# Latent attention in one program: when the stacked query copies are issued, and in which order Pool works

## The chip, the cores and the metric

The kernel runs on one core of a Trainium2 chip. The metric is the device time of one execution in microseconds (us). Engines are named as the profile names them: PE is TensorE's matmul and PEld its weight load, DVE is VectorE, ACT is ScalarE, POOL is GpSimd and SP is SyncE, which here issues DMAs only.

## The reference

One post-norm transformer layer on a sequence of S = 2048 rows of 512 features: multi-head latent attention with 16 heads, a residual and a layer norm, then one linear layer with scale and bias, a residual and a layer norm. Cut to what matters:

```
cq   = rms_norm(x @ w_qa.T)                      # 384 wide
q    = (cq @ w_qb.T)  -> 16 heads x (128 + 64)    # nope part, pe part
q_pe = rope(q_pe)                                 # 64 wide, per head
ckv  = x @ w_kva.T    -> latent 128 (rms_norm), k_pe 64 (rope, shared by all heads)
kv   = latent @ w_kvb.T -> k_nope, v per head
scores = (q_nope @ k_nope.T + q_pe @ k_pe.T) * 192 ** -0.5, causal
out  = softmax(scores) @ v ; x = layernorm(x + out @ w_o.T)
x    = layernorm(x + (x @ (weight * scale[:, None]).T + bias))
```

## The kernel before, in words

**Numbers.** fp32 values go through PE as a high and a low part in a rounded fp32 format, so that each product takes three matmuls. The probabilities are split into two f16 parts (high and low) in the same way. k_nope and v are absorbed: the scores are taken against the shared latent (Kn) and the shared rotary key (Kp), and the values are the latent (V); the heads' value matrices are multiplied into w_o at the end.

**Tiling.** The 16 heads are 8 pairs p. The queries are 4 blocks b of 512 rows, and each block has 4 query tiles qt of 128. In the profiled execution block 0 runs from 0 to about 260 us (with the projections of x and of the weights beside it), block 1 to about 480, block 2 to about 880, block 3 to about 1370; then come the output projection, the norms and the linear layer. The loop in `units` goes over p, qt and (from block 1 on) the two heads j of the pair. Names like (3,6,2) are block, pair, query tile; (0,1,1) beside ring copies is pair, query tile, head in block 1.

**One head (blocks 1 to 3).** `head_scores`: PE computes scores s (L438: three matmuls with Kn, two with Kp, and a mask matmul, L441), DVE takes maxima (L510) and the bias (L517/L518/L520), ACT takes exponentials into a buffer pr (L532) and sums them. `head_probs`: ACT casts pr to f16 (L563), Pool subtracts to get the low part (L564), and `turn` transposes both on DVE back into pr (L546) and issues four SP DMAs (L553) that place them in a ring, `ring<-pr`. `values`, some heads later and in two halves, multiplies the ring's tile with V (L619). In blocks 2 and 3 the result is multiplied by the inverse sums iv (DVE, L628) and stored (ot_d). The inverse comes by a detour through memory: `settle` sums, inverts and turns (DVE, L468, L469, L473), Pool stores it (`rows`, L476), and `values` has Pool load it spread over the partitions (`iv`, L612; the pool of iv has two buffers). In block 0 a pair is processed at once: L598 and L599 are its cast and subtraction.

**The stack.** `project_pe(b, g)` makes the rotary query parts of a group g of four heads. DVE leaves a high part in ph and a low part in prod, both with the heads along the partitions. Eight DMAs of 128 KB each, for head j = 0..3 and part i = high, low, copy 32 partitions at a time into the tile pe, where a head's high part and low part lie one above the other (L393 and L395). `score` reads pe in the matmuls with Kp. A group serves two pairs.

**Putting off.** In block 0 the loads and stores go to Pool's queue (`state["queue"]` is nc.gpsimd). From block 1 on it is nc.sync, and stores and stack copies wait in a list. The list is visited at the end of each `head_probs`, and emptied at the start of each pair:

```python
later.append([n, dst, src])         # put_off(dst, src, n), from block 1 on

def put_in(all=False):
    kept = []
    for n, dst, src in later:
        if n == 0 or all:
            nc.sync.dma_start(dst, src)          # L330
        else:
            kept.append([n - 1, dst, src])
    later[:] = kept
```

**Who sets the order.** In block 0 a scheduler with a planned timeline orders all engines. Engines named in `tc.manual_schedule(engines=...)` keep the program's order instead: PE and SP from block 1 on, DVE and ACT too from (3,0,1) to the end of block 3's hand-over (L729). Pool's order is the planner's throughout. Block 3 also fetches what the output stage needs: `prepare_output` in pairs 6 and 7 loads wv (L871), wo (L862), and two pairs' results with their inverse sums (`latent_load` L823, `latent_rows` L839), and splits them (`latent_split`, L849 on DVE, L64 on ACT, L65 on DVE); `accumulate` (L888) multiplies them.

Of the kernel before, what the change touches and what calls it, by code (L numbers as in the profile page):

```python
# [49 lines left out]
def mla_block(ctx: ExitStack, tc: tile.TileContext, a, out):  # L50
    nc = tc.nc
    ET = mybir.EngineType
# [8 lines left out]
    def split(ps, h, l, scale=None):  # L61

        if scale is None:
            nc.scalar.activation(h, ps, AF.Copy)  # L64
            nc.vector.tensor_tensor(l, ps, h.bitcast(F32), ALU.subtract)  # L65
        else:
            nc.scalar.activation(h, ps, AF.Copy, scale=scale)  # L67
            nc.vector.scalar_tensor_tensor(l, ps, scale, h.bitcast(F32), ALU.mult, ALU.subtract)  # L68
# [124 lines left out]
    def value_output(p, pool, tag):  # L193

        wvo = state["wvo"][p]
        for j in range(2):
            ps = pool.tile([P, HID], F32, tag=tag, name=f"ps_wo{2 * p + j}")
            nc.tensor.matmul(ps, state["wv"][:, 2 * p + j], state["wo"][2 * p + j], start=True, stop=True)  # L198
            split(ps, wvo[:, 0, j, :], wvo[:, 1, j, :], kvln_o)
            yield  # L200
# [118 lines left out]
    def put_off(dst, src, n=0):  # L319

        if state["queue"] is nc.gpsimd:
            nc.gpsimd.dma_start(dst, src)
        else:
            later.append([n, dst, src])
# [9 lines that stand above are left out]
# [20 lines left out]
    def load_wpe(b, g):  # L354
        if b == NB:
            return
        w = state["wpe", b, g] = prj.tile([P, 2, LT, 256], F32R, tag="wpe", name=f"wpe{b}_{g}")
        move(state["queue"], w, wpe_d[g])

    def project_pe(b, g, direct=None):  # L360

        if direct is None and ("wpe", b, g) not in state:
            load_wpe(b, g)
        w = state.pop(("wpe", b, g)) if direct is None else direct
        cq, cs = state["cq"], state["cs"]
        prod = prj.tile([P, 2, 2, QB], F32, tag="prod", name=f"prod{b}_{g}")
        for x in range(2):
            ps = psum["m"].tile([P, QB], F32, tag="m", name=f"ps_pe{b}_{g}_{x}")
            n = 0
            for lt in range(LT):  # L370
                for i, k in ((0, 0), (0, 1), (1, 0)):
                    nc.tensor.matmul(  # L372
                        ps, w[:, i, lt, x * P : (x + 1) * P], cq[:, k, lt, :], start=n == 0, stop=n == 8
                    )
                    n += 1
            for k in range(2):
                nc.vector.tensor_tensor(prod[:, k, x, :], ps, cs[:, k ^ x, :], ALU.mult)
            if x == 0:
                yield
            elif b or g == 3:  # L380
                load_wpe(*((b, g + 1) if g < 3 else (b + 1, 0)))
        rp, tp = prod[:, 0], prod[:, 1]
        nc.vector.tensor_tensor(rp[:, 0, :], rp[:, 0, :], rp[:, 1, :], ALU.subtract)
        nc.vector.tensor_tensor(rp[:, 1, :], tp[:, 0, :], tp[:, 1, :], ALU.add)
        ph, pl = prj.tile([P, 2, QB], F32R, tag="ph", name=f"ph{b}_{g}"), tp.bitcast(F32R)
        split(rp, ph, pl)
        pe = blk.tile([P, 4, QB], F32R, tag="pe", name=f"pe{b}_{g}")

        for j in range(4):
            for i, part in enumerate((ph, pl)):  # L390
                to, src = pe[64 * i : 64 * i + 64, j, :].bitcast(F32), part[32 * j : 32 * j + 32].bitcast(F32)
                if state["queue"] is nc.gpsimd:
                    nc.sync.dma_start(to, src)  # L393
                else:
                    put_off(to, src, 1)  # L395
        state["pe", b, g] = pe
        yield

# [24 lines left out]
    def project(b, p):  # L423
        if p % 2 == 0:
            yield from project_pe(b, p // 2)
        yield from project_nope(b, p)
# [215 lines left out]
    def drain():  # L642
        while fillers:
            fill()
# [48 lines left out]
    def flush():  # L693
        while probs:
            for _ in probs.pop():
                pass

    def units(pool, ring, b):
        lag = min(ring.shape[1] // (2048 * (b + 1)) - 1, 3) if b else 2

        for p in range(NPAIR):
            put_in(True)


            if p + 1 == NPAIR:
                at = (1, 2, 4, 5) if b < NB - 1 else (1, 3, 5, 7)
            elif p % 2 == 0 and p + 2 < NPAIR:
                at = (0, 1, 2, 3) if (b, p) == (1, 0) else (0, 1, 3, 4)
            else:
                at = (3, 4)  # L710
            if b and p % 2 == 0 and p + 2 < NPAIR:
                fillers.append(project_pe(b, p // 2 + 1))
            if p + 1 < NPAIR:
                fillers.append(project(b, p + 1) if b == 0 else project_nope(b, p + 1))
            elif b + 1 < NB:
                fillers.append(project(b + 1, 0))
            if b == NB - 1 and p == NPAIR - 1:
                ctx_p.close()
                pcr = state["pcr"] = ctx.enter_context(
                    tc.tile_pool(name="pcr", bufs=2, side="right", reuse_waits="tile")  # L720
                )
                state["wvo"] = [pcr.tile([P, 2, 2, HID], F32R, name=f"wvo{p}", bufs=1) for p in range(EARLY)]
                for i in range(EARLY):
                    fillers.append(value_output(i, psum["m"], "m"))
                at = (3, 4, 5, 6)
            for qt in range(4):
                nk = (4 * b + qt + 1) * P
                if (b, p, qt) == (NB - 1, 0, 1):
                    ctx_f.enter_context(tc.manual_schedule(engines={ET.PE, ET.SP, ET.DVE, ET.Activation}))  # L729
                if (b, p, qt) == (0, NPAIR - 1, 3):  # L730
                    s0, PT = -4 * nk, prj.tile([P, 4 * nk], F16, tag="ph", name="carry")
                elif b == 0:
                    s0, PT = -4 * nk, pool.tile([P, 4 * nk], F16, tag=f"PT{qt}", name=f"PT{p}_{qt}")
                else:
                    s0, PT = None, place(ring, 2048 * (b + 1), 4 * nk, (b, p) == (2, NPAIR - 1) and qt > 0)
                if nk <= 512:
                    pi = pair_scores(pool, b, p, qt, nk)
                    flush()
                    probs.append(pair_probs(pool, b, p, qt, nk, PT, pi))
                    if qt == 1:  # L740
                        settle((b, p))
                    fill()
                    next(side[0], None)
                    if p and qt % 2:
                        next(side[1], None)
                    if qt % 2:
                        next(side[0], None)
                    run_values(lag)
                    run_values(lag)
                else:  # L750
                    for j in range(2):
                        if 2 * qt + j == 1 if b < 2 else j == 0:
                            settle((b, p))
                        prepare_output(b, p, 2 * qt + j)
                        prev = probs.pop() if probs else iter(())
                        pi = head_scores(pool, b, p, j, qt, nk, prev)
                        probs.append(head_probs(pool, b, j, nk, PT, pi))
                        if (b, p, qt, j) == (1, 0, 1, 0):
                            half_values()
                            half_values()  # L760
                        if 2 * qt + j in at:
                            fill()
                        run_values(lag + (b == 3 and j == 0))
                if b:
                    tile_ = PT.entry
                    tile_[0] = values(b, p, qt, nk, PT)
                    vals.append(tile_)
                else:
                    vals.append([values(b, p, qt, nk, PT), 0, s0, s0 + 4 * nk])
            drain()  # L770
        if b and b < NB - 1:
            flush()
        elif b:
            next(probs[0])
# [20 lines left out]
    def run_values(depth):  # L795

        for _ in range(1 + len(vals) - depth):
            half_values()
# [345 lines left out]
```

## Time and profile before

| | |
|---|---|
| time of three runs | 1638.35, 1634.71, 1636.91 us, median 1636.91 |
| profiled execution | 1638.56 us; its span, first to last instruction, 1636.8 us |
| mean granted clock of TensorE | 0.990 |
| PE busy | 1575.2 us (96%) |
| DVE, ACT, POOL busy | 1130.0 (69%), 918.3 (56%), 846.0 us (52%) |
| subtraction on Pool, L564 | 613.2 us in 320 instructions, mean 1935 ns |
| stack copies pe<-ph and pe<-prod | 64 each, 128 KB, 3.1 and 3.0 us from issue to landing |
| ring copies of 128 KB | 384, 2.9 us |

A row of a timeline has start, duration, engine, line, operation, output tile and input tile, a count of instructions taken together, and in square brackets the idle time before it with what ended it. In a list of waits the three numbers are the sum, the count and the longest. A group's row has the busy time, the mean of one in ns, and the idle time just before them.

### The profile page before, as it was taken

The page shows a single profiled execution, that of the slowest core. Times are in us where ns is not written, and L with a number is a line of the kernel's source. Part 1 is how long each engine was busy: PE and PEld are TensorE (multiplying, and loading weights), DVE is VectorE, ACT ScalarE, POOL GpSimd, SP SyncE. Part 2 cuts the span into 40 slices and gives each one's busy share as a digit, 9 for nine tenths or more (in the row PEclk, how much of TensorE's full clock was granted, in tenths as well). Part 3 has the DMA queues.
Part 4 walks back from the last instruction along what each step waited for, and adds up shares of the span by engine and source line. Part 5 has one row for each costly group of instructions (what it writes and reads, how often), then busy time and mean ns, then how long its engine had stood idle before and what let it go on. Part 6 is the DMA issues. An engine that isn't in the chain of part 4 may idle for free. (4 is left out here: it accounts for less than half of the span.)

```text
span 1636.8 us, 27536 instructions
## 1 busy us (share of the span) xinstructions
PE 1575.2 (96%) x9292; PEld 1294.5 (79%) x9292; DVE 1130.0 (69%) x1874; ACT 918.3 (56%) x1529; POOL 846.0 (52%) x701
## 2 busy tenths in 40 slices
PE   9799998899999999999999999999999998999998
PEld 7688876788888888888887778888887776678876
DVE  5668665577677777777777678778677676575464
ACT  5557564666665757666665665666666654321120
POOL 2345553454554766667765566666666665011011
PEclk9899999999999999999999999999999999999999
DMA  6988676676776878787787767867777777962030
GB/s 213 265 238 267 194 203 164 175 185 172 191 206 171 217 179 202 162 206 181 199 195 180 177 153 174 184 160 160 177 156 192 211 178 210 320 197 77 32 117 33
DMA packets 259436, 297.60 MB, mean 182 GB/s; under 512 B 35264, under 2 KB 227136, under 8 KB 258272
## 3 DMA queue, kind: packets, MB, share of 16 engines
q1 hardware_dynamic: 241008, 251.63, 55.4%
q0 software_dynamic: 11376, 34.52, 12.0%
q10 hardware_dynamic: 6912, 9.70, 2.0%
q8 instruction: 74, 1.21, 0.3%
q14 instruction: 66, 0.54, 0.1%
HBM read 99.94 MB, written 36.44 MB: 83 GB/s over the span
## 5 line engine op out<-in xcount | busy, mean ns | idle before, releaser
L564 POOL TENSOR_TENSOR hlpr<-pr,hlpr 128x1024 f16<-128x1024 f32 (+3 forms) x320 | 613.2, 1935 | 327.2 <-ACT hlpr L563 297.9
L438 PE MATMUL s<-Kn,qn 128*128 128x512 f32 (+4 forms) x1920 | 510.3, 373 | 22.3 <-ACT pr L532 13.9
L532 ACT ACTIVATE pr<-s,bias,rq 128x1024 f32<-128x1024 f32 (+3 forms) x320 | 325.4, 1021 | 343.2 <-issue 178.3
L510 DVE TENSOR_REDUCE neg<-s 128x1 f32<-128x1024 f32 (+3 forms) x320 | 310.0, 985 | 133.2 <-PE s L441 75.0
L438 PEld LDWEIGHTS s<-Kn,qn 128*128 128x128 f32 x1920 | 334.3, 189 | 72.7 <-ACT pr L532 19.9
L619 PE MATMUL o<-ring,V 128*128 128x256 f16 x3024 | 373.1, 273 | 7.4 <-DMA ring<-pr 5.3
L546 DVE STREAM_TRANSPOSE pr<-hlpr 128x1024 f32<-128x1024 f32 (+7 forms) x256 | 311.5, 1223 | 97.9 <-POOL hlpr L564 72.2
L438 PE MATMUL s<-Kp,pe 128*128 128x512 f32 (+4 forms) x1280 | 362.9, 364 | 5.5 <-DMA pe<-prod 5.5
L619 PEld LDWEIGHTS <-V 128*128 128x128 f16 x3264 | 301.1, 96 | 82.7 <-issue 32.0
L563 ACT ACTIVATE hlpr<-pr 128x1024 f16<-128x1024 f32 (+3 forms) x320 | 338.2, 1113 | 4.9 <-DVE pr L546 1.0
L438 PEld LDWEIGHTS s<-Kp,pe 128*128 128x128 f32 x1280 | 233.6, 189 | 36.4 <-DMA pe<-prod 5.7
L410 PE MATMUL ps_qn<-cq,wq 128*128 128x512 f32 x576 | 150.0, 405 | 2.1 <-DMA wq<-wq_d 1.9
L989 POOL TENSOR_TENSOR lnr<-lnt,nhalf 128x1 f32<-128x1 f32 x32 | 21.3, 671 | 213.3 <-DVE lnt L988 213.2
L410 PEld LDWEIGHTS ps_qn<-cq,wq 128*128 128x128 f32 x576 | 105.5, 192 | 23.1 <-DVE xl L65 1.1
L68 DVE SCALAR_TENSOR_TENSOR qn<-ps_qn,kvln,qn 128x512 fp32r<-128x512 f32 x64 | 47.5, 744 | 45.5 <-ACT qn L67 45.2
L599 POOL TENSOR_TENSOR hl<-pr,hl 128x128 f16<-128x128 f32 (+3 forms) x64 | 56.8, 908 | 37.7 <-ACT hl L598 37.3
L372 PE MATMUL ps_pe<-cq,wpe 128*128 128x512 f32 x288 | 75.3, 407 | 0.2 <-DMA cq<-cq_d 0.2
L64 ACT ACTIVATE oh<-o 128x1024 fp32r<-128x1024 f32 x28 | 29.7, 1061 | 79.6 <-PE acc L888 49.1
L888 PE MATMUL acc<-wvo,oh 128*128 128x512 f32 x224 | 71.5, 401 | 1.0 <-ACT pr L532 0.6
L64 ACT ACTIVATE xt<-tp 128x512 fp32r<-128x512 f32 x16 | 9.6, 598 | 94.8 <-PE tp L1008 94.8
L532 ACT ACTIVATION_READ_ACCUMULATOR pr<-s,bias,rq 128x1 f32 x320 | 61.8, 193 | 0.0
L372 PEld LDWEIGHTS ps_pe<-cq,wpe 128*128 128x128 f32 x288 | 53.4, 193 | 10.6 <-issue 0.3
(458 smaller groups left out, 1777.4 us busy)
## 6 DMA issues: line engine op xcount, KB each, us to landing
ring<-pr SPq DMA_DIRECT2D x384, 128.0 KB, 2.9
wq<-wq_d SPq DMA_DIRECT2D x22, 768.0 KB, 6.7
ring<-pr SPq DMA_DIRECT2D x128, 112.0 KB, 3.4
o<-ot_d SPq DMA_DIRECT2D x28, 512.0 KB, 5.5
ot_d<-ot SPq DMA_DIRECT2D x97, 128.0 KB, 2.7
ring<-pr SPq DMA_DIRECT2D x128, 96.0 KB, 2.4
ring<-pr SPq DMA_DIRECT2D x64, 192.0 KB, 4.1
ring<-pr SPq DMA_DIRECT2D x64, 176.0 KB, 5.3
```

Source lines behind the costliest of these rows:

```text
L68: nc.vector.scalar_tensor_tensor(l, ps, scale, h.bitcast(F32), ALU.mult, ALU.subtract)
L372: nc.tensor.matmul(ps, w[:, i, lt, x * P : (x + 1) * P], cq[:, k, lt, :], start=n == 0, stop=n == 8)
L410: nc.tensor.matmul(ps, w[:, i, lt, j * P : (j + 1) * P], cq[:, k, lt, :], start=n == 0, stop=n == 8)
L438: nc.tensor.matmul(ps[:, :w], lhs, K[:, i, c0 : c0 + w], start=n == 0, stop=n == 4 and not by_product)
L510: nc.vector.tensor_reduce(neg[:, ti : ti + 1], v, axis=AX.XY, op=ALU.max, negate=True)
L532: nc.scalar.activation(pr[:, x : x + n * w].rearrange("p (a c) -> p a c", a=n), v, AF.Exp, bias=bias, scale=r, accum_out=sums_of(b, p, qt, ...
L546: nc.vector.transpose(sq.rearrange("p (k c r) -> p k c r", k=4, r=32), words.rearrange("p (c k r) -> p k c r", k=4, r=32))
L563: nc.scalar.activation(hl[:, 0, c], pr[:, c], AF.Copy)
L564: nc.gpsimd.tensor_tensor(hl[:, 1, c], pr[:, c], hl[:, 0, c], ALU.subtract)
L599: nc.gpsimd.tensor_tensor(hl[:, j, 1, :], pr[:, j, :], hl[:, j, 0, :], ALU.subtract)
L619: nc.tensor.matmul(ps[:, :256], vt[:, i, k % 4, :], v[:, :, l, k, :], start=n == 0, stop=n == 3 * kts - 1)
L888: nc.tensor.matmul(acc, l[:, t, c], state["wvo"][p][:, i, j, :], start=p == 0 and j == 0 and n == 0, stop=p == NPAIR - 1 and j == 1 and n ...
```

## The change

Three places are edited.

```diff
@@ project_pe, L390
             for i, part in enumerate((ph, pl)):
                 to, src = pe[64 * i : 64 * i + 64, j, :].bitcast(F32), part[32 * j : 32 * j + 32].bitcast(F32)
                 if state["queue"] is nc.gpsimd:
-                    nc.sync.dma_start(to, src)
+                    (nc.sync, nc.gpsimd)[i].dma_start(to, src)
                 else:
-                    put_off(to, src, 1)
+                    put_off(to, src, 1 + j)
@@ units, L726
                 if (b, p, qt) == (NB - 1, 0, 1):
-                    ctx_f.enter_context(tc.manual_schedule(engines={ET.PE, ET.SP, ET.DVE, ET.Activation}))
+                    ctx_f.enter_context(tc.manual_schedule(engines={ET.PE, ET.SP, ET.DVE, ET.Activation, ET.Pool}))
```

In block 0 the copies of the low part are issued by Pool and those of the high part by SP, as before; with the first group of block 1, which block 0 prepares, these are five groups of eight copies. In blocks 1 to 3 the two copies of head j are held back for 1 + j visits of the list instead of all eight for one, so that they go out two at a time, behind the ring copies of successive heads. From (3,0,1) on Pool executes in the program's order, as the other engines do. In the program's order of a query tile of block 3, Pool has the two subtractions of the tile's first head, the iv of an earlier tile, the rows store, and the two subtractions of the second head. The computation is the same.

## The prediction

> **What bounds the kernel now.** I read the page's busy times first, then the clock row, then TensorE's chain of waits, then the timelines around each of its longest idle times. On this kernel a change of about 0.2% (3.3 us) is the least that a measurement can tell from none.
>
> ```profile
> PE 1575.2 (96%) x9292; PEld 1294.5 (79%) x9292; DVE 1130.0 (69%) x1874; ACT 918.3 (56%) x1529; POOL 846.0 (52%) x701
> ...
> PEclk9899999999999999999999999999999999999999
> ```
> TensorE (PE) is busy for 1575.2 of 1636.8 us, so only some 62 us of idle time, and what the few slices below 9 in the clock row add, can be won at all. Its waits:
>
> ```profile
> engine line waited for: us in total, times, longest us
> PE s L438 <- ACT pr L532: 13.9, 10, 2.3
> ...
> PE s L438 <- DMA pe<-prod: 5.5, 1, 5.5
> PE o L619 <- DMA ring<-pr: 5.3, 1, 5.3
> ```
> Two single waits concern the copies that the change touches: one of 5.5 us for a stack copy and one of 5.3 us for probabilities. The 13.9 us in ten waits for exponentials are where Pool could matter. By stretch, TensorE is busy 159.41 of the 160 us in 320-480, 399.71 of 400 in 480-880 and all 280 in 960-1240; it is not full in 120-240 (114.17 of 120), 240-320 (67.94 of 80), 880-960 (73.64 of 80) and 1240-1370 (120.49 of 130). An edit earns time only there.
>
> **The stack copies in blocks 1 to 3 (delay 1 + j).** SP's timeline:
>
> ```profile
> 280.52 0.61 SPq L330 DMA_DIRECT2D pe<-ph  x1
> ...
> 285.04 0.60 SPq L330 DMA_DIRECT2D pe<-prod  x1
> 285.68 0.58 SPq L330 DMA_DIRECT2D ot_d<-ot  x1
> 286.51 0.56 SPq L59 DMA_DIRECT2D wq<-wq_d  x1
> 287.17 10.10 SPq L553 DMA_DIRECT2D ring<-pr  x12
> ```
> and TensorE's:
>
> ```profile
> 288.84 0.23 PE L441 MATMUL s<-maskb,identb 128*128 128x128 bf16 x1
> 294.33 2.08 PE L619 MATMUL o<-ring,V 128*128 128x256 f16 x9 [5.27 <-DMA ring<-pr]
> ```
> Eight copies hold SP from 280.52 to 285.64, then come a store, a 768 KB load, and only at 287.17 the four ring copies of head (0,1,1), though VectorE had transposed that head by 283.00 (row 282.03 0.97). They land between 293.17 and 293.98, and TensorE stands for 5.27 us. By the order of the changed program only the two copies of j = 0 stand before this head's ring copies. Six issues of 0.645 us spacing leave the way: 3.87 us. 287.17 - 3.87 = 283.30, just after the transpose, so all of it counts. The nine matmuls after the wait took 2.08 us and the nine of 298.39 took 1.16; a wait of 1.4 us instead of 5.27 should save that 0.9 as well. Against this, the other six copies now stand two by two before the ring copies of (0,2,0), (0,2,1) and (0,3,0), while TensorE arrives earlier; I give back 0.5. Sum -4.3. Bounds: -6 if the slow restart reaches further than nine matmuls and nothing is given back; -2 if the ring copies still queue behind the 768 KB load (6.40 us to landing) and the next head is late by 2.
>
> In every later group the same spreading happens while TensorE is full, and the idle time left there is 0.59 and 0.29 us. A copy of j = 3 goes out three heads later than now, or at the next pair's start at the latest, and lands after 3.1 us; a group serves two pairs, so it stays ahead of use. -0.5, between -1 and 0.
>
> **The low halves on Pool's queue in block 0.** Five groups of four copies move from SP to Pool, the last being block 1's first group:
>
> ```profile
> 247.50 1.86 SPq L393 DMA_DIRECT2D pe<-ph  x3
> 249.95 1.83 SPq L393 DMA_DIRECT2D pe<-prod  x3
> ```
> ```profile
> 249.15 0.85 POOL L59 DMA_DIRECT2D wq<-wq_d  x1
> ```
> ```profile
> 257.77 0.90 PE L438 MATMUL s<-Kp,pe 128*128 128x320 f32 x2 [5.48 <-DMA pe<-prod]
> ```
> The low half of j = 0 is issued at 249.95 and lands at 257.73, beside a 768 KB load on Pool's queue (249.15 to 259.04). In the changed order Pool issues that load, then half a subtraction (3.29 us for two in the row of 244.25, so 1.65), then the four low copies: the first at 249.15 + 0.85 + 1.65 = 251.7, behind the load in one queue. If the load lands in the 6.6 us that such loads of Pool take in the median, at 255.8, and the copy 1.2 later, it is at 257.0, a gain of 0.7; if the copy takes its 7.78 us again it is at 259.5, a loss of 1.8. Nearer to the second row, since the same bytes are moving: +0.8, bounds -0.7 and +1.8.
>
> A row speaks against this edit too: a 128 KB ot_d store lands 3.5 us after its issue from Pool and 2.7 us from SP. The Trainium skill ("DMA: Bandwidth & Descriptors", section "Issuing engines are not separate DMA queues") says that all issuing engines feed the same 16 DMA engines, so that spreading issues saves the sequencer's issue time and no more. By that rule alone this boundary would be worth nothing and the sum would be 0.8 us better than mine; by the two rows of 3.5 and 2.7 it is a loss.
>
> For the four other groups SP is freed of 4 x 0.6 = 2.4 us each, and Pool takes 4 x 0.55 = 2.2 us each (the issue row of ot_d at 251.74), with subtractions of the probabilities (L599, 908 ns each) queued behind them and behind VectorE's low half. In 120-240 Pool is busy 70.25 of 120 us, so 2.2 us per group has room. But a planner orders all engines in block 0, and the change alters its whole listing. TensorE idles 5.8 us in 120-240, so I put this at 0, between -4 (most of that idle time goes) and +4 (half of the 8.8 us of Pool issues reaches TensorE).
>
> **Pool in program order from the second query tile of block 3.** The gate before is the store and load of the inverse sums on Pool:
>
> ```profile
> 1302.86 0.76 POOL L612 DMA_DIRECT2D iv<-rows(3, 6, 2)_14852  x1 [2.24 <-DVE neg L510]
> ...
> 1309.01 1.25 DVE L546 STREAM_TRANSPOSE pr<-hlpr 128x1024 f32<-128x1024 f32 x1 [1.68 <-POOL hlpr L564]
> ...
> 1313.15 1.21 ACT L532 ACTIVATE pr<-s,bias,rq 128x1024 f32<-128x1024 f32 x1 [3.77 <-DVE bias L518]
> ```
> The planner put iv early; it waits for its buffer (about 39 us of such waits in 880-1370), and the subtractions L564 wait behind it. VectorE then transposes late, takes the next maximum late, ScalarE waits 3.77 us for the bias and TensorE 1.6. I replayed Pool's queue in the changed order with the durations of this trace, each subtraction starting no earlier than its cast (L563) ended, each rows store no earlier than its inverse (L473). The subtractions of a tile's first head then end 0.8 us earlier before the wait at 945 (2.5 us on TensorE), 2.1 us before the one at 1312 (1.8) and 0.6 before the one at 1360 (2.4). Each shift reaches TensorE as far as its wait goes: -0.8 - 1.8 - 0.6 = -3.2. iv is issued later, but still, with 3 us for its landing, at least 2.3 us ahead of the multiply that reads it.
>
> The largest wait there has another cause. Between 1280.18 and 1282.74 the planner issues five large loads on Pool's queue (o, iv, o, iv, wo); ring copies issued beside them take 11.71 to 14.52 us, an exponential waits 4.86 us for its buffer, and TensorE 2.3. In program order these loads stand at about 1324, 1329 and 1338, two at a time. I count -2.3 and +1.0 for a milder jam there: -1.3.
>
> Against both: the rows store now stands ahead of both subtractions of the tile's second head, before it stood ahead of one, and it waits for VectorE's inverse. In the replay these subtractions end up to 2.8 us later in (3,5,1), 2.6 in (3,6,0) and 3.3 in (3,7,0), where the loads of o and iv also stand before them; only the last two lie where TensorE has no reserve. Of their 5.9 us I take a quarter, +1.5, since an earlier first head also brings the inverse earlier. Sum for block 3: -3.2 - 1.3 + 1.5 = -3.0, between -5.5 (nothing late reaches TensorE, no new jam) and +2.7 (all 5.9 does, and the new jam costs what the old did).
>
> **The hand-over to the output.** At its end Pool's program order puts o_3, iv_2 and iv_3 (512 KB each) before the iv of (7,2), which went first at 1368.51. In the replay they are issued at 1379.9 to 1381.2 and that iv at 1382.0. The split L849, which waited 3.89 us and ran at 1383.87, moves some 4 us; its user on TensorE runs at 1396.35, about 9 us behind the split's end. The multiply of (7,2), at 1388.41, moves to about 1393. +1.5, between 0 (all covered) and +4.
>
> **Sum.** -4.3 - 0.5 + 0.8 + 0 - 3.0 + 1.5 = -5.5. The profiled execution took 1638.56 us in all (1.8 beyond its span), 1.65 above the median of the three runs: 1636.91 - 5.5 = 1631.4.
>
> **Rivals.** *Slower: the rows stores at the head of Pool's queue.* All lateness of the replay outside TensorE's full stretches reaches it: 2.4 in 880-960 and 1.3 + 2.6 + 0.6 + 2.5 + 3.3 + 0.6 = 10.9 in 1240-1370, 13.3 together. With the jam gone (-1.3) block 3 is +12 and the sum -4.3 - 0.5 + 0.8 + 12 + 1.5 = +9.5: 1646. It decides for slower once more than about half of the 13.3 arrives. For it: one late inverse now holds a whole head of Pool's work. Against: before, Pool waited as long for iv, and TensorE was full through 960-1240. *No change.* The wait of 5.27 us moves on to (0,2,1), leaving -2, the shifts of Pool are taken up by other waits (0), boundary and hand-over cost 0.8 + 1.5: about 1637. For it: the DMA engines are 65% busy in 240-320, and a 768 KB load still stands before the ring copies. *More.* Block 0's new order gains its 4 us besides: 1627.
>
> **Chances.** Forecast 0.55 (0.46 faster by over 0.2%, 0.09 within), more gain 0.09, no change 0.16 (0.02, 0.10 and 0.04 slower), rows stores 0.20 (all slower). Together 0.57 faster, 0.19 same, 0.24 slower. The range is 1623 to 1643: it takes in the gain's bound for block 0 and for 288.84 together, and reaches halfway into the slower case.
>
> **What would show it.** Right: ring copies of (0,1,1) issued near 283.3 after two copies, the wait of 5.27 below 2; no iv waits in Pool's queue in block 3; no ring copy of over 10 us near 1285. Wrong: a wait at 258 grown past 7.5 us, waits for hlpr grown on VectorE with TensorE idle more than 9.5 us in 1240-1370, or TensorE below 114 us in the stretch 120-240.

## The result, and the profile after

The changed kernel took 1656.17 us in the median (1652.15 to 1657.66), the kernel before 1637.22 us: a ratio of 1.0107, with an interval of 1.008 to 1.0134. By the ratio it is slower by 17.5 us. Two more measurements of the same kernel, beside other kernels, gave 1.0066 (1.0041 to 1.0091) and 1.0078 (1.0058 to 1.0098). The forecast was 5.5 us faster. Single executions of one kernel scatter (before: 1632 to 1646 us), which matters for everything below that rests on one profile.

The page of the changed kernel, the busy times and TensorE's clock:

```profile
PE 1583.0 (96%) x9292; PEld 1301.7 (79%) x9292; DVE 1137.8 (69%) x1874; ACT 918.0 (55%) x1529; POOL 855.9 (52%) x721
...
PEclk9899998999999999999999999999999999999999
```

The span is 1655.9 us, so TensorE is idle for 72.9 us, 11 more than before. The other 8 us are busy time: the same 9292 matmuls took longer, at a mean granted clock of 0.983 against 0.990 (a second slice of the clock row, at 248 to 290 us, is below 9). Its chain of waits (sum, count, longest):

```profile
PE o L619 <- DMA PT<-pr: 9.6, 2, 5.0
...
PE ps_wo L207 <- DVE ot L628: 6.3, 1, 6.3
PE s L438 <- ACT pr L532: 5.1, 4, 2.3
...
PE ps_pe L372 <- DVE prod L377: 3.2, 1, 3.2
PE s L438 <- DMA pe<-prod: 3.0, 4, 1.3
...
PE o L619 <- DMA ring<-pr: 2.2, 1, 2.2
```

The wait for the ring copies has shrunk from 5.3 to 2.2 us, and the waits for exponentials in blocks 1 to 3 fell from 13.9 to 5.1. The single wait of 5.5 us for a stack copy, where block 1 begins, is gone: the 3.0 us are four short waits, only 0.6 of them at that place. But just ahead of it TensorE now waits about as long for the last probabilities of block 0, so the boundary has gained nothing:

```profile
270.25 2.08 PE L619 MATMUL o<-PT,V 128*128 128x256 f16 x9 [4.99 <-DMA PT<-pr]
```

What is new stands elsewhere: the other 4.6 of the 9.6 us for copies of block 0's probabilities, 6.3 us at the hand-over, 3.2 us on a product of the query projection. By the start times of equal instructions, the changed kernel is 15.9 us late when block 1 begins, the same at its end, 21.4 late through most of block 2, 17.8 late at 963 us, about 17 in the middle of block 3, 14.2 at block 3's last maximum and 19.1 at the end.

### The profile page after: what moved, and what is told of

It is laid out like the page before. It is cut to its first block, busy times and chain, and to the rows that moved or that the text cites. A ratio compares the mean times of both kernels' runs of the same rounds, so it can differ in the third digit from the quotient of the medians.

```text
span 1655.9 us, 27544 instructions
## 1 busy us (share of the span) xinstructions
PE 1583.0 (96%) x9292; PEld 1301.7 (79%) x9292; DVE 1137.8 (69%) x1874; ACT 918.0 (55%) x1529; POOL 855.9 (52%) x721
## 4 chain that ended last, share of the span: by engine, by line
PE 73%; DMA 11%; DVE 5%; issue 4%; POOL 3%; SPq 2%; ACT 2%; ACTq 0%; DVEq 0%; POOLq 0%
PE s L438 31%; PE o L619 17%; PE acc L888 9%; PE ps_qn L410 6%; PE ps_pe L372 3%; DMA ring<-pr 2%; POOL hlpr L564 2%; PE ff L1022 2%; SPq L553 2%; DMA pe<-prod 1%; PE ps_cq L271 1%; DVE pr L546 1%; DMA ot_d<-ot 1%; DMA PT<-pr 1%; PE s L441 1%
## 5 line engine op out<-in xcount | busy, mean ns | idle before, releaser
L67 ACT ACTIVATE qn<-ps_qn,kvln 128x512 fp32r<-128x512 f32 x64 | 43.7, 683 | 34.3 <-PE ps_qn L410 34.0
```

## The experiments

Every kernel ran against before on the same chip; the ratio with its interval decides on time. Each kernel has one profile, and stages are compared over groups of kernels that share an edit, because executions of the same listing differ by several us in a stage.

### The edits alone: e1_split, e2_delay, e3_pool, and the last two together: e4_delay_pool

```diff
e1_split:       (nc.sync, nc.gpsimd)[i].dma_start(to, src)      # block 0 only
e2_delay:       put_off(to, src, 1 + j)
e3_pool:        manual_schedule(engines={..., ET.Activation, ET.Pool})
e4_delay_pool:  e2_delay and e3_pool
```

> Only the first edit: in block 0 the low halves' copies go out on Pool's queue. Theory A (the loss is made in block 0, by the planner's new listing with Pool's queue in it): the 32 maxima of block 0 are late as in the changed kernel (+8 us at pair 4, +16 to +18 at pair 7), block 1 starts about 16 us late, and the time is 14 to 20 us above before. Theory B (the loss is spread: the first edit costs at most what I had allowed, +4, and the rest comes from Pool's order and the delays): 0 to +5 us.

> Only the second edit: put_off(to, src, 1 + j). My prediction's term: the wait of 5.3 us at 289 shrinks below 2 and nothing new appears, -3 to -5 us. Theory A from the two traces: the wait at 289 is split over two later ring groups (3.1 and 2.4 us in the changed kernel), so 0 to -2 there, and the delayed copies of the last heads of block 1 cost 4 to 5 us at its end (near 520 to 535): +2 to +5 us in all.

> Only the third edit: Pool in the program's order from (3,0,1). My prediction: -3 us in block 3 and +1.5 at the hand-over, about -1.5. Theory A from the two traces: block 3 gains about 3 us in 880 to 960 and 4 to 7 in 1245 to 1340, and the hand-over loses 4 to 6: -2 to -7 us in all. The rival of the prediction (rows stores at the head of Pool's queue) wants +5 or more.

> The second and third edits without the first. If the three edits add up, this is the changed kernel less the cost of the first: about 0 to -3 us against before (theory A), or -6 (my prediction's terms). Theory B wants most of the 19 us here: +10 or more.

Measured: e1_split 1.0035 (1.0018 to 1.0051), e2_delay 0.9994 (0.9973 to 1.0015), e3_pool 1.0055 (1.0036 to 1.0075), e4_delay_pool 1.0012 (0.9995 to 1.0029). None is faster. The first edit costs 5 to 6 us. In time that is the top of theory B; in its trace block 1 begins 15.7 us late, as theory A had it. The second cannot be told from no change (-4.4 to +2.5 us), between the prediction's -3 to -5 and theory A's +2 to +5. The third alone costs 9, where all but the rival expected a gain; with the second beside it, about 2, a little above theory A's 0 to -3.

In the trace of e3_pool TensorE waits twice for exponentials, 0.7 to 1.5 us each, a few us after each of pairs 1, 3 and 5 of block 3 begins (before 954 and 961, 1077 and 1084, 1199 and 1207 us), and the stretch of 963 to 1250 takes 291.4 us, against 287.7 in e4_delay_pool. This is the time of the prediction's rival, but its mechanism does not show there: the subtractions ahead of these waits wait 5.2 to 6.5 us for the cast and not for a rows store, and ahead of the casts ScalarE waits 2.2 to 4.0 us for ring copies to land. In e4_delay_pool, where the stack copies are spread, the six waits are absent, so the two edits seem to meet there. One profile each does not prove it: f2_pool_tail below, with spread copies, has two of the six (1.3 and 0.7 us).

### Do they add up: a0_all, e12_split_delay, a5_all

```diff
a0_all, a5_all:    the whole change again
e12_split_delay:   e1_split and e2_delay
```

> The changed kernel again, beside kernels with fewer edits on the same chip. The single runs so far gave +5.0 us for the first edit alone and +2.3 for the second and third together, 7.3 in sum, where the whole change gave +18. If the edits add up, this run shows about +7 to +8; if they do not, +16 to +19 again, and the missing 10 us must be found in a stage where two edits meet.

> First and second edit, Pool as before. If the edits add up: +5.0 - 1.3 = about +4. If the first and the second meet (the gain of the second near 289 was missing in the changed kernel: 0.0 there against -3.8 and -4.7 us without the first edit): +8 to +10.

> The changed kernel in five rounds. If the edits add up with their stage costs in the traces (block 0 about +11, the start of block 2 +6, the hand-over +7, less 4 at 289, 4 in 880 to 963 and 4 in 1240 to 1340): +10 to +12 us. If the first measurement holds: +16 to +18.

Measured: a0_all 1.0066, a5_all 1.0078 (intervals above), e12_split_delay 1.0077 (1.0052 to 1.0102), that is +10.8, +12.8 and +12.6 us. The parts do not quite add up: a0_all lies between the 7 to 8 us of the sum and the 16 to 19 of the first measurement, a5_all a little above the 10 to 12 that the stages gave, and e12_split_delay well above its 4 and even above the 8 to 10 of edits that meet. The first measurement of +17.5 was not met again; its interval begins at 13 us and overlaps those of the two later ones.

The stages by group, in us (one profile each; "end" is the time from block 3's last maximum to the last instruction; q_order is left out of the first two rows, g_pool_early of the last three, h_ot of the last):

| stage | kernels with the edit | kernels without it | difference of means |
|---|---|---|---|
| begin to block 1's first maximum, edit 1 | 273.7 to 276.6 (6 kernels) | 260.2 to 268.8 (12) | +11.8 |
| around the wait at 289, edit 2, no edit 1 | 18.6 to 22.7 (9) | 22.8 to 23.3 (3) | -3.1 |
| start of block 2, edit 2 for all groups | 34.2 to 35.8 (6) | 28.6 to 29.2 (13) | +6.3 |
| 1250 to 1295 in before, edit 3 | 36.6 to 36.8 (8) | 40.4 to 44.2 (10) | -5.7 |
| 1295 to 1338 in before, edit 3 | 46.2 to 48.5 (8) | 42.7 to 45.4 (10) | +3.6 |
| end, edit 3 | 272.0 to 275.3 (7) | 265.2 to 270.2 (10) | +5.6 |

### Where block 0's 12 us come from: q_last, q_first, q_order

```diff
q_last:   (nc.sync, nc.gpsimd)[i * b].dma_start(to, src)         # only block 1's first group
q_first:  (nc.sync, nc.gpsimd)[i * (1 - b)].dma_start(to, src)   # only block 0's four groups
q_order:  all eight copies on SP, four high halves first, then four low ones (block 0)
```

> Of the first edit only the last group: the low halves of block 1's first group, which block 0 prepares, go out on Pool's queue; the four earlier groups stay on SP. TensorE's order of instructions is that of before. Theory C (the loss of about 11 us in block 0 is the planner's new listing of TensorE's work, not the queue): block 0 is as before up to 245 us and the boundary moves by -3 to +2; time within 3 us of before. Rival D (Pool's queue is what costs, where the four copies and the 768 KB load stand behind each other): the wait near 252 grows to 7 or 8 us, +2 to +4 us.

> The first edit for the four groups that block 0 itself uses, the last group staying on SP. TensorE's listing is the same as with the whole first edit. Theory C (the listing): as the whole first edit, +4 to +7 us, with the stage of pair 6 (214 to 230 in before) longer by 7 us. Rival D (the last group's queue): 0.

> No copy leaves SP; in block 0 the eight copies of a group are only issued in another order, the four high halves and then the four low ones, as in the changed kernel's listing for SP but all on one queue. This too makes the planner list block 0 anew (206 lines of TensorE's order differ, 142 in the changed kernel). Theory C: the new listing alone moves block 0's end by several us, up or down, with Pool's queue untouched. Rival D: block 0's end stays within the scatter of the unedited listing (0 to +5 us of the profiled run of before).

Measured: q_last 0.9999 (0.9984 to 1.0014), q_first 1.0033 (1.0016 to 1.005), q_order 1.0023 (1.0008 to 1.0038). In time the last group is worth nothing, as theory C said, though the interval reaches to +2.3 us; the trace has the sign of rival D, a wait for the stack copy of 7.99 us where block 1 begins (5.0 to 7.8 in the eleven other kernels with the same listing). The four earlier groups carry the whole cost of the edit (block 1 begins at 276.6 us, in q_last at 267.1). And a mere reordering of the copies on SP, with nothing on Pool, costs 3.8 us of time. Its block 0 ends at 268.7 us, at the upper edge of what the old listing shows, so that its trace alone would not decide; the ratio does. A new order thus costs several us without Pool's queue. But it does so in another place: in q_order pair 6 takes 15.8 us, as before, and pair 7 takes 35.9 (28.3 to 33.4 in the other kernels), with a wait of 11.08 us for copies of probabilities that go out behind the last group's copies.

What the listing does can be read in pair 6, the longest loss: of the 11.8 us, 6.9 arise there, 5.8 in pairs 0 to 5, where they were not traced to a wait, and pair 7 gives 0.8 back. Pair 6 takes 14.0 to 15.7 us in the twelve kernels with the old listing and 22.2 to 22.7 in five of the six with the new one (18.0 in a5_all). TensorE before, where values of pair 6 stand behind the scores of pair 7:

```profile
226.56 0.29 PE L441 MATMUL s<-maskb,identb 128*128 128x128 bf16 x2
...
234.12 0.29 PE L441 MATMUL s<-maskb,identb 128*128 128x128 bf16 x2
234.24 0.82 PE L619 MATMUL o<-PT,V 128*128 128x256 f16 x6
```

and in the changed kernel, where the same six matmuls come first:

```profile
237.34 0.28 PE L441 MATMUL s<-maskb,identb 128*128 128x128 bf16 x2
242.21 1.46 PE L619 MATMUL o<-PT,V 128*128 128x256 f16 x6 [4.58 <-DMA PT<-pr]
```

In both kernels copies of these probabilities are slow beside the loads of block 1's cq (1.5 MB) and of wq (768 KB) that Pool has just issued: 8.8 to 9.6 us to landing before (four copies, issued at 223.41 to 225.31), 9.03 for the last copy in the changed kernel (issued at 233.14, the load of cq at 233.16). Before, TensorE has three groups of scores to work on in that time; after, it waits 4.58 us, and the six matmuls then take 1.46 us instead of 0.82. In q_first it is the same wait:

```profile
PE o L619 <- DMA PT<-pr: 4.4, 1, 4.4
```

The sixth kernel with this listing, a5_all, shows what the wait is worth: there the last copy goes out 0.7 us ahead of the load of cq, lands after 4.79 us, TensorE does not wait, and pair 6 takes 18.0 us.

What stays open is the balance: block 1 begins 11.8 us late in the mean, while e1_split and q_first cost 5 to 6 us in time. Their stages after block 0 are shorter than those of before's profile, and partly than those of q_last; one profile each does not settle why. Part of it is at the end, which takes 265.2 to 267.1 us in the three kernels with the first edit and without the third, and 268.0 to 270.2 in the seven with neither.

### Why spreading the copies gains nothing: f1_delay_g, f1_again

```diff
-                    put_off(to, src, 1 + j)
+                    put_off(to, src, 1 + j if g else 1)
```

> The second edit for groups g = 1 to 3 only; the first group of a block keeps put_off(to, src, 1). Theory: the 6.7 us that the second edit costs at the start of block 2 come from the tile prod, of which there is one buffer: VectorE's next product (L377, second group) waits until the delayed copy of j = 3 has landed (36.23 after 35.74 in us from 500 in the changed kernel). Groups 0 and 1 of a block follow each other closely, the others do not. Then this kernel keeps the gain at 289 (-4) and has no wait on L377 at the start of block 2: -4 to -6 us against before. Rival: the 6.7 us come from the ring copies pushed back by the spread copies; then the loss shrinks no more than a little, and the time stays within 2 us of the second edit alone.

> The kernel f1 again (the second edit for groups 1 to 3 only), to settle whether it is faster than before: -6 to -10 us as in its first run (-9.9), or -3 to -5 if that was scatter and only the stage near 289 is gained.

Measured: 0.9946 (0.9927 to 0.9965) and 0.9964 (0.9952 to 0.9976), so 6 to 9 us faster than before (the theory had 4 to 6), and faster than the second edit alone. The theory's place is confirmed: the start of block 2 takes 28.6 and 28.9 us again (35.4 in e2_delay), and the stage around 289 keeps its gain (19.3 and 20.6 against 23.3). That stage accounts for some 3 to 4 us; where the rest of the gain arises is open. The lines of the changed kernel show the mechanism, on SP, on VectorE and on TensorE:

```profile
533.48 0.60 SPq L330 DMA_DIRECT2D pe<-prod  x1
```
```profile
536.30 1.29 DVE L377 TENSOR_TENSOR prod<-ps_pe,cs 128x512 f32<-128x512 f32 x2 [3.70 <-issue]
```
```profile
537.65 3.11 PE L372 MATMUL ps_pe<-cq,wpe 128*128 128x512 f32 x9 [3.20 <-DVE prod L377]
```

The copy of j = 3 is issued at 533.48, behind four heads' ring copies, and lands at 536.23. Its source is the tile prod, which has one buffer, and the next group's product, which writes prod, starts at 536.30. In all six kernels with the second edit for every group this product starts 0.08 us after that copy lands. VectorE's queue stands meanwhile, and TensorE waits for that product, which reads its accumulator. Group 0 of a block is made in the last pair of the block before and group 1 in the first pair of the block, so their products follow each other closely; between the others lie two pairs or more, and there the copies may well be late. In f1_again's chain of waits the product no longer appears, and the waits for copies are the one where block 1 begins and two near 293 and 300 us:

```profile
PE s L438 <- DMA pe<-prod: 5.3, 1, 5.3
...
PE o L619 <- DMA ring<-pr: 3.9, 2, 2.0
```

### Where Pool's order loses: f2_pool_tail, g_pool_early, h_tail, h_ot, f1_ot

```diff
f2_pool_tail:  f1, Pool in program order, and at the hand-over:
-  latent_load(0, EARLY + 1, nc.gpsimd.dma_start); latent_rows(0, EARLY + i, nc.gpsimd.dma_start)
+  latent_load(0, EARLY + 1, nc.sync.dma_start);   latent_rows(0, EARLY + i, nc.sync.dma_start)
g_pool_early:  f1, Pool in program order from (3,0,1) to the end of pair 5 only
h_tail:        f1, Pool in program order; o_3 loaded right after o_2; settle() behind latent_rows
h_ot:          h_tail, and ot of (7,3) in a buffer of its own
f1_ot:         f1, and ot of (7,3) in a buffer of its own
```

> The kernel f1 with Pool in the program's order and, at the hand-over, the load of o_3 and the two loads of inverse sums (iv_2, iv_3) issued by SP instead of Pool. Theory: the 7 us that the third edit loses at the hand-over come from these three loads, which stand before the iv of (7,2) on Pool's queue. Without them that iv is issued 3 us earlier and alone, the multiply L628 of (7,2) and (7,3) comes 6 to 7 us earlier, and the time is 2 to 4 us below f1 (block 3's own -5.7 and +3.9). Rival: the loads jam the DMA engines wherever they are issued; then the hand-over stays 5 to 7 us late and the time is 3 to 5 us above f1.

> The kernel f1 with Pool in the program's order from (3,0,1) up to the end of pair 5 only; from pair 6 on the planner orders Pool again, as before. Theory: the gain in 1240 to 1295 (-7) and the losses behind it (+4 in 1295 to 1340, +7 at the hand-over) all come from where the large loads for the output stage stand in Pool's order, in pairs 6 and 7, and none from the rows stores; then this kernel is within 2 us of f1. Rival (the rows stores at the head of Pool's queue): +2 us or more against f1, with TensorE idle in 960 to 1240.

> The kernel f1 with Pool in the program's order, where o_3 is loaded together with o_2 (in pair 7) and, at the hand-over, iv_2 and iv_3 are issued before the last rows store instead of behind it. Theory: the hand-over is late because the split L849 of (0,2) waits for iv_2 (9 to 11 us in the changed kernel and in f2) and the multiply L628 of (7,2) stands behind it on VectorE; iv_2 issued some 3 us earlier, without o_3 before it, takes 4 us or more of the 7 back, and the time is 3 to 5 us below f2 (which was 3 us below before). Rival: the iv of (7,2), still issued after those loads, is what ot of (7,2) waits for; then the hand-over stays at +6 to +7.

> The kernel h_tail with a buffer of its own for ot of (7,3), so that this multiply does not wait for the store of (7,1) to land. Theory (the store's landing is the gate): the wait of TensorE on L628 (4.5 us in h_tail) is gone or below 1, the time is 4 to 5 us below h_tail's ratio of 0.9979, near 0.995. Rival (the iv of (7,3) or the slow loads of wo are next in line): the multiply comes at most 2 us earlier, ratio 0.997 to 0.998.

> The kernel f1 with the same buffer. In its run TensorE waited 2.1 us there; at most that is gained: ratio 0.995 to 0.997 (f1: 0.9946 and 0.9964), the difference to f1 being hard to tell.

Measured: f2_pool_tail 0.9982 (0.9964 to 1.0), g_pool_early 1.001 (0.999 to 1.003), h_tail 0.9979 (0.9964 to 0.9994), h_ot 0.9957 (0.9937 to 0.9977), f1_ot 0.9951 (0.9926 to 0.9977).

*The rows stores of pairs 0 to 5 cost nothing in g_pool_early.* There only these pairs have Pool's program order, and the stretch of 963 to 1250 us takes 287.5 us, as in before (287.5) and in f1 (287.3 and 286.7). But the kernel is some 9 us slower than f1 all the same, which the expectation of 2 us missed; the time is the rival's, without the idle TensorE in 960 to 1240 that it wanted. The planner, taking over at pair 6, now lists the loads of wv and of two iv tiles together at 1237 to 1239 (7.5 to 12.8 us to landing). Ring copies land late behind them, an exponential waits for its buffer, and TensorE for the exponential:

```profile
ACT pr L532 <- DMA ring<-pr: 16.4, 3, 9.1
```
```profile
1253.36 1.56 PE L438 MATMUL s<-Kn,qn 128*128 128x512 f32 x3 [4.30 <-ACT pr L532]
```

So in this kernel the place of the large loads decides, not the order of the subtractions. In the changed kernel they stand apart on Pool's queue, and later than before:

```profile
1335.35 0.53 POOL L823 DMA_DIRECT2D o<-ot_d  x1
1335.88 0.76 POOL L839 DMA_DIRECT2D iv<-inv_d  x1
1340.53 0.55 POOL L823 DMA_DIRECT2D o<-ot_d  x1
1341.08 0.77 POOL L839 DMA_DIRECT2D iv<-inv_d  x1
```

They land within 5.7 to 7.2 us (5.2 to 14.1 before). That gains 5.7 us where they used to stand and costs 3.6 where they are now; TensorE's longest wait in the second place is one of 2.4 us before 1351, for VectorE, on a weight product (L198).

*The hand-over loses 5.6 us.* VectorE before:

```profile
1383.87 1.23 DVE L849 TENSOR_TENSOR o<-o,iv 128x1024 f32<-128x1024 f32 x1 [3.89 <-DMA iv<-inv_d]
...
1401.54 0.42 DVE L628 TENSOR_TENSOR ot<-o,iv 128x256 f32<-128x256 f32 x1 [6.64 <-DMA ot_d<-ot]
```

VectorE and TensorE in the changed kernel:

```profile
1404.16 1.23 DVE L849 TENSOR_TENSOR o<-o,iv 128x1024 f32<-128x1024 f32 x1 [9.12 <-DMA iv<-inv_d]
...
1407.70 0.42 DVE L628 TENSOR_TENSOR ot<-o,iv 128x256 f32<-128x256 f32 x1
...
1424.12 0.42 DVE L628 TENSOR_TENSOR ot<-o,iv 128x256 f32<-128x256 f32 x1 [7.63 <-DMA ot_d<-ot]
```
```profile
1424.60 2.07 PE L207 MATMUL ps_wo<-wo,wv 128*128 128x512 f32 x2 [6.25 <-DVE ot L628]
```

The split L849 waits 9.12 us for iv_2 (before: 3.89), the multiply of (7,1) stands behind it in VectorE's order, its store goes out late into the jam of loads (4.6 us after the multiply, since SP sits 4.78 us on the load of o ahead of it, 1.40 before), and the multiply of (7,3) waits for that store, since there are two buffers for ot. Before, the last link is there too, but TensorE waits only 0.92 us for it. The multiply of (7,2) waits besides for its iv, 13.58 us from issue to landing (5.66 before). Moving the three loads to SP (f2_pool_tail) did not help, as the rival had it (6.8 us above f1_delay_g on the same chip, where it said 3 to 5): SP issues them behind the last head's ring copies, iv_2 lands later still and the split waits 11.29 us. In h_tail iv_2 is early again, and the first link is mended, the last not:

```profile
1374.38 1.22 DVE L849 TENSOR_TENSOR o<-o,iv 128x1024 f32<-128x1024 f32 x1 [3.88 <-DMA iv<-inv_d]
...
1395.48 0.42 DVE L628 TENSOR_TENSOR ot<-o,iv 128x256 f32<-128x256 f32 x1 [10.25 <-DMA ot_d<-ot]
```

The theory of h_tail fell: its time is that of f2_pool_tail. With a buffer of its own for that ot (h_ot) the wait of TensorE on L628 is gone, but a new one stands a little later:

```profile
PE acc L890 <- DVE ol L65: 4.2, 1, 4.2
```

It comes from a load of o, for which VectorE waits 11.2 us. From the last maximum to the end h_ot takes 273.3 us, h_tail 274.5 and f1 269.1 and 270.2: only 1.2 us came back in these profiles, within the rival's 2. The ratio, 0.9957, lies between the theory's 0.995 and the rival's 0.997 to 0.998, and its interval holds both. So the buffer is at most a part of it; that the loads together bind the hand-over is likely and not shown, and which of them would have to move is left open. In f1_ot the end takes 270.1 us, as without the buffer, and its time is that of f1.

## Why the prediction was wrong, step by step

- **Block 0, put at 0 between -4 and +4: this step failed.** It measured +11.8 us at block 1's first maximum (5 to 6 us in the time of the edit alone), and the prediction's own sign came: TensorE is busy for 109.09 us of the stretch 120-240, below 114. The bounds came from the wrong sizes, TensorE's idle time and half of Pool's issue time. The prediction said that the planner lists all engines anew and then priced only the 20 copies. In pair 6, where more than half of it arises, the cost is the place of other work: values taken ahead of scores, while a copy of theirs is slow beside a 1.5 MB load that stands there in both kernels. The rows to bound this with were there: copies of 8.8 to 9.6 us at 223, hidden by three groups of scores. Without that cover TensorE waits 4.4 to 4.6 us in five of the six kernels. The 5.8 us of pairs 0 to 5 stay open.
- **The later groups, put at -0.5: failed.** The start of block 2 costs +6.3 us. "A group serves two pairs, so it stays ahead of use" looked at the reader of pe alone. The other end of the copies, the tile prod with its one buffer, and its next writer L377 were not asked about. This alone turns the second edit from a gain into nothing.
- **The wait at 289, put at -4.3, from -6 to -2: right mechanism and right size.** Without the first edit it is -3.1 in the mean (-2.7 to -4.7 for nearly all kernels). The ring copies of (0,1,1) stand behind two stack copies, and what is left is 0.8 to 2.3 us, in most kernels twice; the second wait was not in the sum. In the profile of the changed kernel itself the stage gained nothing: the 768 KB load ahead of the ring copies took 7.92 us to land (6.40 before, 5.39 in e4_delay_pool), and two waits of 2.9 and 2.2 us remained (the first is listed under VectorE, but the ring copies landed 0.14 us before it ended).
- **The boundary, put at +0.8 between -0.7 and +1.8: not contradicted.** q_last has the edit there only, and its ratio is 0.9999, within -2.6 to +2.3 us. Its profile has the wait that the prediction named as a sign of being wrong, 7.99 us; a kernel without the edit has 7.76, so this is no proof of a loss. The rule of the Trainium skill weighed there ("DMA: Bandwidth & Descriptors", section "Issuing engines are not separate DMA queues") gave 0, and the ratio agrees with it; the row of ot_d (3.5 against 2.7 us), which spoke for a loss, did not decide.
- **Block 3, put at -3.0: right in direction, near in size partly by luck.** The signs came but for a rest: of 39 us of iv waits in Pool's queue one of 2.9 is left, and no ring copy there takes over 8.5 us. The stretch with the jam of loads gained 5.7 us and the next one lost 3.6, together -2.1, where the prediction had -2.3 and +1.0 for the two jams and the rest from shifts of the subtractions. These shifts cannot be told from the differences between executions, and the stretch of 880 to 963 gives no verdict; the waits they were to shorten are 2.3, 1.6 and 2.3 us in the profile, not 2.5, 1.8 and 2.4. The rival of the rows stores, +13.3 us, did not happen: between 963 and 1250 the changed kernel takes 287.7 us, before 287.5. That holds with the second edit beside it; the third edit alone lost 3.9 us there.
- **The hand-over, put at +1.5 between 0 and +4: too small.** It measured +5.6 (group means). The step followed iv_2 and the split to their user on TensorE and found 9 us of room there. It did not follow VectorE's order behind the split: the multiply of (7,1), its store, and the multiply of (7,3) that waits for the store's buffer.
- **The chances.** The slower case had 0.24, with the rows stores as its only mechanism. The time came from three other places, two of which the prediction had priced at about nothing.

## What to carry to other kernels

A copy that is issued later holds its source as well as its target: before delaying one, find the next writer of the source and the number of its buffers (here the one-line limit to groups 1 to 3 turns no gain into one of 6 to 9 us). Where a planner lists the engines, an edit of a few DMAs is to be priced by what a new listing may put behind a known slow transfer, and not only by the cost of those DMAs; compare the two listings around each transfer that only neighbouring work hides. When a load moves later in a queue, follow the in-order engine behind its first reader down to the last store, for a later link of the chain may be a buffer that this store frees.

The version to keep is f1, which leaves block 0 and Pool's order as they were: 0.9946 and 0.9964 of before in two measurements.

## What the runs showed of the hardware

The same 768 KB load near 289 took 5.39 and 7.92 us to land in two kernels with the same DMAs before and behind it on the queues (e4_delay_pool and the changed kernel); the stage behind it took 18.6 and 23.4 us. A copy of 128 KB issued by Pool was not slow in itself: four low halves issued at 157.84 to 159.41 us of the changed kernel took 3.24 to 4.67 us, at 0.52 us from one issue to the next, where SP's copies take 0.65. And block 0 ended between 260.2 and 268.8 us over twelve executions with one listing, with up to 4.9 us of it between 162 and 176 us; a term of 4 us in that stage cannot be read from one profile.
